# Regrouping the neighbour scores: eight rows with all 64 places per step instead of 32 rows with 16, and the relu of the fourth head on ScalarE

## The chip, the cores and the metric

The kernel runs on one core of one Trainium2 chip. The metric is the device time of one execution in microseconds (us). A core has five engines that run side by side, each through its own instructions in order: TensorE (PE, with its weight loads listed as PEld), VectorE (DVE), ScalarE (ACT), GpSimd (POOL) and SyncE (SP). Sixteen DMA engines move data between HBM and the on-chip memory SBUF. PE writes its results into PSUM, which is divided into eight banks of 2 KB per partition; DVE and ACT read them from there.

## The reference

Two graph layers work on 3327 nodes with 128 features. The adjacency `adj` is a sparse 3327 x 3327 matrix with some 64 non-zeros per row, its diagonal among them. Each layer normalises its input, applies a relu and adds its result to its input. Layer 0 is an attention layer with four heads; layer 1 is a graph convolution with the same adjacency.

```python
def _gatv2_head(x, A_shape, w1, w2, a, Wlin):
    x1 = x @ w1
    x2 = x @ w2
    E = jax.nn.leaky_relu(x1[:, None, :] + x2[None, :, :], negative_slope=0.01)
    s = E @ a
    s = jnp.tanh(s / 8.0) * 8.0
    s = jnp.exp(s) * A_shape
    s = s / jnp.sum(s, axis=-1, keepdims=True)
    out = s @ x @ Wlin.T
    return jax.nn.leaky_relu(out, negative_slope=0.01)
...
# layer 0: x = x + concat(heads) @ w        layer 1: x = x + relu(D^-1/2 (A+I) D^-1/2 (h @ W.T + b))
```

A score is needed only where `A_shape` is not zero. For one row i and one neighbour j, the score of a head is the sum over 128 features of `a * leaky_relu(x1[i] + x2[j])`. The leaky relu is 0.01 times its input plus 0.99 times a relu, and the linear part is a sum of two numbers, one of the row and one of the neighbour. What is left to be done for each pair is the relu of 128 features in four heads.

## The kernel before

The rows are worked on in 26 blocks of 128. A block has two halves of 64 rows (`hb`). For every row, `prep` (L353) finds the column numbers of its non-zeros with MAX8 and MATCH_REPLACE8 on DVE and puts the first 64 into 64 *places*; the few that are left over go into an extra list. The places come in four chunks of 16. `idx` holds for each chunk and each set of eight rows the 128 addresses (8 rows x 16 places) of the table rows to be fetched. A table row holds, besides adjacency values, the features of a node, one partial score per head, and its `x2` for the four heads.

`gather` (L578) fetches: one indirect DMA on POOL (L597) brings 128 table rows into one *tile* `g[:, t]`, one row to a partition. Eight tiles make one buffer `g`; there are four buffers. In the kernel before, a buffer `w` (0 to 3) holds chunk `w` of all 64 rows of the half: tile `t` is rows 8t to 8t+7. The extra entries and the rows' own entries on the diagonal have a buffer of their own, `ge`.

The scores are worked out in *groups* `m`, nine to a half. Groups 0 to 7 are four tiles each, two groups to a buffer; so a group is 32 rows with 16 places. Group 8 is for `ge`. A group goes through these steps:

- `stage_z` (L612): for each pair of heads `hp`, PE transposes the four tiles of both heads (L624, eight transposes) into a PSUM tile `z` of two banks, one per head, in which the columns stand in the order (32 rows, 16 places). DVE then writes `r = max(z, -x1)` for both heads in one instruction of 1024 columns (L640); `x1n` holds `-x1`, and the same number is used for the 16 columns of a row. Since `max(z, -x1)` is `relu(z + x1) - x1`, the score's number of the row, `pex`, makes up for the difference. Two `z` tiles exist, so a `z` can be written again only when its `r` is done.
- `stage_r` (L645), one group later: four matmuls, one per head, multiply `r` with `a` and write into two rows per head of the PSUM tile `s` (L653). The two groups of a buffer fill one `s`.
- `finish` (L657), once per buffer: ACT copies `s` into `ssb` (L662); DVE makes `wq` (L666) from the adjacency values; PE turns `ssb` back (L671); DVE adds the partial scores of neighbour and row (L674, L677); ACT takes tanh and exp (L682, L684); DVE multiplies with `wq` into `wt` (L693); PE adds the weighted features of the neighbours into `ag` (L702). In L702 the eight tiles write into four strips of 32 PSUM partitions each (`cg`), and neighbouring matmuls are for different strips.

After L702 the buffer is free (`allow("g")`), and the next eight gathers may go out on POOL. `close` (L727) finishes a half.

The order of all this is written out by hand. The loop at L1195 emits, for group i, first `stage_z` of group i, then `stage_r` of group i-1. Between the parts it calls `slot()` (L858), six times per group. Each call goes one step further in `finish` and `close` (a `yield` is a step), in the search for the next block's columns (`prep`, with L422, L453, L456 on DVE and the transposes L365 of the adjacency with their ACT copies L367), and sends off gathers (`fetch`, `trickle`). Every engine takes its instructions in that order. A branch at the end that recomputes everything densely is not taken.

## Time and profile before

| What | Number |
|---|---|
| Median of 14 runs | 3397.97 us (3374.82 to 3404.78) |
| The profiled execution | 3400.7 us, span 3399.0 us, instructions 52430 |
| Mean granted TensorE clock | 0.897 |
| Busy: PE / DVE / ACT / POOL | 2652.0 / 2107.0 / 673.5 / 1739.4 us |
| DVE, `r` of groups 0 to 7 (L640) | 832 instructions, 1012.0 us |
| PE, transposes into `z` (L624) | 6656 matmuls, 1048.8 us |
| PE, `ag` (L702) | 3328 matmuls, 206.7 us |
| POOL, gathers of `g` (L597) | 1664, 1615.1 us |
| DMA | 826.94 MB, 619.41 MB of it by POOL's gathers |

The profile is of one execution. "Busy" is the time in which an engine works on an instruction; matmuls overlap one another, and their ends are modelled, so that a busy PE is not PE at its peak. A group of instructions is shown as: line, engine, operation, out<-in, shape, how often, and then the busy time, the mean of one in ns, and the idle time of the engine ahead of it with what ended it. A matmul with 32-bit operands shows as two records (L702: 208 x 8 matmuls, 3328 records); a transpose is one. "Issue" is time in which the engine waited for nothing that the profile shows, and "remote" is a wait whose end the profile can't put down to an instruction.

### The profile page before, as it was taken

To read this page: it belongs to the slowest core of one execution; us is meant where nothing else is said; L and a number is where in the kernel's file an instruction comes from. 1 tells how busy PE (TensorE), PEld (TensorE's weight loads), DVE (VectorE), ACT (ScalarE), POOL (GpSimd) and SP (SyncE) were. 2 spreads that over 40 slices of the span, in tenths; PEclk is the share of its full clock that TensorE was granted. 3 is DMA by queue.
4 is the path that set the end of the run, shared out by engine and by line. 5 is a ranking of instruction groups with operands and counts; after the bars stand their busy time and mean duration, and the time that the engine had idled before them with its cause. 6 is when DMAs were issued, how large, how long until landed. Compare 5 with 4: busy or idle time off the path is not lost.

```text
span 3399.0 us, 52430 instructions
## 1 busy us (share of the span) xinstructions
PE 2652.0 (78%) x19410; PEld 1785.4 (53%) x19410; DVE 2107.0 (62%) x6478; ACT 673.5 (20%) x1703; POOL 1739.4 (51%) x1822
## 2 busy tenths in 40 slices
PE   6578778787777877877778778787788787788887
PEld 4355555555555555555555555555555555555553
DVE  6567666666666666666665665666665666665442
ACT  3122112112211211212221121121121121121110
POOL 3555555555555555555555545555455455455520
PEclk8789888988988988999898888899898899899998
DMA  9977778678778767877767867877776776777896
GB/s 326 310 257 240 219 259 267 217 245 273 224 230 264 247 215 245 270 222 238 263 214 245 263 199 247 269 226 231 241 244 213 239 239 222 239 240 222 262 269 174
DMA packets 417844, 826.94 MB, mean 243 GB/s; under 512 B 38435, under 2 KB 288815, under 8 KB 414255
## 3 DMA queue, kind: packets, MB, share of 16 engines
q0 software_dynamic: 141440, 619.41, 55.8%
q1 hardware_dynamic: 165343, 147.87, 13.8%
q10 hardware_dynamic: 110800, 56.25, 5.7%
q8 instruction: 156, 2.56, 0.3%
q14 instruction: 105, 0.86, 0.1%
HBM read 754.47 MB, written 113.22 MB: 255 GB/s over the span
## 4 chain that ended last, share of the span: by engine, by line
PE 47%; DVE 21%; another core or an unknown queue 14%; issue 8%; DMA 4%; ACT 3%; POOL 1%; ACTq 0%; SPq 0%; DVEq 0%
PE z L624 16%; DVE r L640 10%; PE s L653 9%; PE tr L671 4%; PE z L629 3%; DVE cand L422 2%; PE ag L702 2%; DMA g<-table,idx 2%; PE tr L379 1%; PE ag L721 1%; PE tr L365 1%; POOL g L597 1%; DVE cand L456 1%; ACT r L637 1%
## 5 line engine op out<-in xcount | busy, mean ns | idle before, releaser
L597 POOL DMA_INDIRECT g<-table,idx x1664 | 1615.1, 971 | 1395.4 <-PE ag L702 826.7
L624 PE MATMUL z<-ident,g 128*128 128x128 f32 x6656 | 1048.8, 304 | 305.8 <-DVE r L640 223.0
L640 DVE TENSOR_TENSOR r<-z,x1n 128x1024 f32<-128x1024 f32 x832 | 1012.0, 1218 | 394.6 <-remote 302.5
L624 PEld LDWEIGHTS z<-ident,g 128*128 128x128 f32 x6656 | 861.9, 158 | 530.4 <-DVE r L640 329.2
L653 PE MATMUL s<-r,sel 128*2 128x512 f32 (+1 forms) x3744 | 558.4, 601 | 21.5 <-issue 12.0
L671 PE MATMUL tr<-ident,ssb 128*128 128x128 f32 x988 | 181.8, 311 | 172.5 <-issue 101.4
L662 ACT COPY ssb<-s 128x512 f32<-128x512 f32 x260 | 147.2, 566 | 721.2 <-PE s L653 338.7
L702 PE MATMUL ag<-g,wt 128*32 128x133 f32 x3328 | 206.7, 285 | 86.2 <-issue 82.7
L702 PEld LDWEIGHTS ag<-g,wt 128*32 128x32 f32 x3328 | 121.5, 112 | 259.4 <-issue 242.8
L674 DVE TENSOR_TENSOR sc<-tr,g 128x32 f32<-128x32 f32 x208 | 39.1, 188 | 319.3 <-remote 144.1
L671 PEld LDWEIGHTS tr<-ident,ssb 128*128 128x128 f32 x988 | 123.6, 156 | 208.9 <-issue 123.6
L422 DVE MAX8 cand<-codes 128x8 f32<-128x52 uint16 x1664 | 215.2, 204 | 0.0
L635 DVE TENSOR_TENSOR r<-z,x1n 128x128 f32<-128x128 f32 x104 | 27.6, 287 | 240.7 <-PE s L653 191.3
L682 ACT ACTIVATE th<-sc 128x32 f32<-128x32 f32 x260 | 58.1, 223 | 596.3 <-DVE sc L677 308.6
L367 ACT COPY at<-tr 128x512 f32<-128x512 f32 (+1 forms) x175 | 97.4, 556 | 344.2 <-remote 149.4
L597 POOL DMA_INDIRECT ge<-table,idxo x104 | 100.7, 968 | 113.5 <-PE ag L721 52.1
L653 PEld LDWEIGHTS s<-r,sel 128*2 128x2 f32 x3744 | 58.1, 82 | 185.3 <-issue 176.8
L379 PE MATMUL tr<-at,x_sb 128*128 128x128 f32 x488 | 80.8, 310 | 90.8 <-ACT at L367 65.8
L629 PE MATMUL z<-oi,x1b 128*128 128x256 f32 x416 | 145.4, 431 | 0.0
L453 DVE MAX8 lists<-cand 128x8 f32<-128x272 f32 (+1 forms) x338 | 133.2, 394 | 2.9
L365 PE MATMUL tr<-ident,adjb 128*128 128x128 f32 x676 | 113.0, 291 | 25.2 <-DMA adjb<-in_adj_dram 16.9
L379 PEld LDWEIGHTS tr<-at,x_sb 128*128 128x128 f32 x488 | 67.0, 210 | 115.6 <-ACT at L367 96.1
(201 smaller groups left out, 2624.3 us busy)
## 6 DMA issues: line engine op xcount, KB each, us to landing
adjb<-in_adj_dram SPq DMA_DIRECT2D x26, 1664.0 KB
table<-AT_d SPq DMA_DIRECT2D x26, 1664.0 KB
AT_d<-at ACTq DMA_DIRECT2D x150, 256.0 KB
g<-table,idx POOLq DMA_INDIRECT x1664
table<-img SPq DMA_DIRECT2D x12, 1296.0 KB
adjb<-AT_d SPq DMA_DIRECT2D x72, 128.0 KB
g<-AT_d SPq DMA_DIRECT2D x25, 256.0 KB
g<-AT_d ACTq DMA_DIRECT2D x25, 256.0 KB
```

Of the source, the lines that this page charges most:

```text
L365: nc.tensor.transpose(pt[:, q, :], adjb[:, (j0 + q) * P:(j0 + q + 1) * P], ident)
L379: nc.tensor.matmul(pq[:, :P], x_sb[:, j0 + q, :], at[:, q, :], start=(q == 0), stop=(q == js[-1]))
L422: nc.vector.max(cand[:, c, 8:].rearrange("p (r s) -> p r s", s=32)[:, :, sgm % 32], codes.rearrange("p a b -> p (a b)")[:, sgm % 32 * SEG: ...
L453: nc.vector.max(top, of)
L597: return nc.gpsimd.indirect_dma_start(out=g[:, t, lo:hi], out_offset=None, in_=tab, in_offset=bass.IndirectOffsetOnAxis(ap=at[:, t:t + 1], ...
L624: nc.tensor.matmul(z[:, i, q * P:(q + 1) * P], g[:, m % 2 * 4 + q, c0:c0 + D], ident, is_transpose=True, start=(q == 0 or m < 8), stop=(m ...
L629: nc.tensor.matmul(z[:, i, :n], k.x1b[:, h * D:(h + 1) * D], k.oi[:, hb * n:(hb + 1) * n], start=False, stop=True, skip_group_check=True)
L640: nc.vector.tensor_tensor(r.rearrange("p h (i s) -> p h i s", s=16), z.rearrange("p h (i s) -> p h i s", s=16), k.x1n[:, 2 * hp:2 * hp + 2 ...
L653: nc.tensor.matmul(k.s[32 * h:32 * h + 2, :n], sel[:, h, 31 - at:33 - at], rs[h // 2][:, h % 2, :n], start=(at == 0), stop=(at == 1 or m = ...
L662: nc.scalar.copy(ssb[:, :nk * P], s[:, :nk * P])
L671: nc.tensor.transpose(pt[:, q, :], ssb[:, q * P:(q + 1) * P], ident)
L702: nc.tensor.matmul(ag[32 * cg:32 * cg + 32, u, :WORK], wt[:, t].rearrange("p h q -> p (h q)"), g[:, t, f0:f0 + WORK], start=(w == 0 and t ...
```

## The change

Three things change, in five places.

1. *What a buffer and a group hold.* Buffer `w` now holds all four chunks of 16 rows instead of one chunk of 64 rows. Its tile `4m+q` is chunk `q` of rows 16w+8m to 16w+8m+7. A group is then eight rows with all 64 places. The gathers are as many, and each brings the same 128 table rows as before for its chunk and rows; only the order is different (`own` and `which` in `gather`). In `z` the columns are put in the order (8 rows, 64 places): each transpose writes its 128 columns as eight runs of 16, 64 columns apart. `finish` undoes this when it copies `s` into `ssb` on ACT, by reading `s` in another order.
2. *The relu of the fourth head.* Since one row now has 64 columns next to each other, DVE's instruction for the second pair of heads covers only the third head (512 columns), and ACT does the fourth in eight instructions of 64 columns, `relu(z + x1)` with the row's `x1` as a bias per partition. `prep` makes a second copy of `x1` without the minus sign (`x1p`, on ACT), and `pex` of the fourth head takes the other row score (two DVE instructions instead of one), because that head's `r` no longer lacks `x1`.
3. *The order of the matmuls into `ag`.* A tile's strip is now that of its rows, `(2w+m) % 4`. A buffer holds only two sets of eight rows, so its eight tiles write into two strips instead of four, and neighbouring matmuls alternate between those two.

```diff
--- before.py
+++ after.py
@@ -559,16 +559,19 @@
                 nc.tensor.matmul(pm[:, h * P:(h + 1) * P], w1_sb[:, h, :], hTb, start=True, stop=True)
             x1n = pb.tile([P, H, P], F32, name="x1n")
             nc.scalar.activation(x1n, pm[:, :H * P].rearrange("p (h i) -> p h i", h=H), AF.Copy, scale=-1.0)
+            x1p = pb.tile([P, P], F32, name="x1p")
+            nc.scalar.copy(x1p, pm[:, (H - 1) * P:H * P])
             pmx = pb.tile([P, 16, H], F32, name="pmx")
-            nc.vector.tensor_tensor(pmx, tmask[:, :, None].to_broadcast([P, 16, H]),
-                                    p_all[:, b, None, :H].to_broadcast([P, 16, H]), OP.mult)
+            for h0, h1, of in ((0, H - 1, 0), (H - 1, H, H)):
+                nc.vector.tensor_tensor(pmx[:, :, h0:h1], tmask[:, :, None].to_broadcast([P, 16, h1 - h0]),
+                                        p_all[:, b, None, of + h0:of + h1].to_broadcast([P, 16, h1 - h0]), OP.mult)
             yield
             yield
             pm = bank()
             nc.tensor.matmul(pm[:, :16 * H], modsel, pmx.rearrange("p t h -> p (t h)"), start=True, stop=True)
             pex = pb.tile([P, 16, H], F32, name="pex")
             nc.scalar.copy(pex, pm[:, :16 * H].rearrange("p (t h) -> p t h", h=H))
-            k.x1b, k.x1n, k.pex = x1b, x1n, pex
+            k.x1b, k.x1n, k.x1p, k.pex = x1b, x1n, x1p, pex
             yield
 
         def rows_in():
@@ -588,14 +591,18 @@
                 c0, n0 = (0, FEAT + COLS) if hb == 0 else (FEAT, BODY + FEAT)
                 nc.sync.dma_start(g[:HALF, FOUND, :n0], tables[b % 2][:NP * ROW].rearrange("(r c) -> r c", c=ROW)[rows:rows + HALF, c0:c0 + n0])
             else:
-                g, n, at = rows_in(), WT, k.idx[:, w, WT * hb:WT * hb + WT]
+                g, n, at = rows_in(), WT, k.idx
+
+            t0 = WT * hb + 2 * w
 
             def one(t):
+                own = 8 * (2 * w + t // 4)
+                which = at[:, t % 4, t0 + t // 4:t0 + t // 4 + 1] if w < NW else at[:, t:t + 1]
                 lo, hi = (0, FEAT + COLS) if hb == 0 else (0, BODY + FEAT)
                 if w < NW:
-                    lo, hi = (8 * t, hi) if hb == 0 else (0, BODY + 8 * t + 8)
+                    lo, hi = (own, hi) if hb == 0 else (0, BODY + own + 8)
                 return nc.gpsimd.indirect_dma_start(out=g[:, t, lo:hi], out_offset=None, in_=tab,
-                                                    in_offset=bass.IndirectOffsetOnAxis(ap=at[:, t:t + 1], axis=0))
+                                                    in_offset=bass.IndirectOffsetOnAxis(ap=which, axis=0))
 
             queue.extend((k, hb, w, partial(one, t)) for t in range(n))
             k.g[hb, w] = g
@@ -621,7 +628,8 @@
                     h = 2 * hp + i
                     c0 = k.f0[hb] + PROJ + h * D
                     for q in range(n // P):
-                        nc.tensor.matmul(z[:, i, q * P:(q + 1) * P], g[:, m % 2 * 4 + q, c0:c0 + D], ident,
+                        to = z[:, i, q * P:(q + 1) * P] if m == 8 else z[:, i].rearrange("p (i q s) -> p q i s", q=4, s=16)[:, q]
+                        nc.tensor.matmul(to, g[:, m % 2 * 4 + q, c0:c0 + D], ident,
                                          is_transpose=True, start=(q == 0 or m < 8), stop=(m < 8), skip_group_check=True)
                     if m == 8:
                         nc.tensor.matmul(z[:, i, n:n + HALF], g[:HALF, FOUND, c0:c0 + D], ident[:HALF, :HALF],
@@ -636,9 +644,14 @@
                                             k.x1n[:, 2 * hp:2 * hp + 2, HALF * hb:HALF * hb + HALF], OP.max)
                     nc.scalar.activation(r[:, :, :n], z[:, :, :n], AF.Relu)
                 else:
-                    r0 = HALF * hb + 32 * (m % 2)
-                    nc.vector.tensor_tensor(r.rearrange("p h (i s) -> p h i s", s=16), z.rearrange("p h (i s) -> p h i s", s=16),
-                                            k.x1n[:, 2 * hp:2 * hp + 2, r0:r0 + 32, None].to_broadcast([P, 2, 32, 16]), OP.max)
+                    r0 = HALF * hb + 8 * m
+                    nh = 2 - hp
+                    nc.vector.tensor_tensor(r[:, :nh].rearrange("p h (i s) -> p h i s", s=HALF), z[:, :nh].rearrange("p h (i s) -> p h i s", s=HALF),
+                                            k.x1n[:, 2 * hp:2 * hp + nh, r0:r0 + 8, None].to_broadcast([P, nh, 8, HALF]), OP.max)
+                    if hp:
+                        for e in range(8):
+                            nc.scalar.activation(r[:, 1, e * HALF:(e + 1) * HALF], z[:, 1, e * HALF:(e + 1) * HALF], AF.Relu,
+                                                 bias=k.x1p[:, r0 + e:r0 + e + 1], scale=1.0)
                 out.append(r)
             return out
 
@@ -659,11 +672,15 @@
             f0 = k.f0[hb]
             nt, nk, nm = (WT, 4, 2) if w < NW else (OVT, OVT, 1)
             ssb = ph.tile([P, BANK], F32, name="ssb", bufs=1)
-            nc.scalar.copy(ssb[:, :nk * P], s[:, :nk * P])
+            if w < NW:
+                nc.scalar.copy(ssb.rearrange("p (q i s) -> p q i s", q=4, s=16), s.rearrange("p (i q s) -> p q i s", q=4, s=16))
+            else:
+                nc.scalar.copy(ssb[:, :nk * P], s[:, :nk * P])
             if w < NW:
                 wq = pb.tile([P, WT, 8], F32, name="wq")
-                diag = bass.AP(g.tensor, g.offset + BODY * hb, [list(g.ap[0]), [WIDE + 8, 8], [1, 8]])
-                nc.vector.tensor_tensor(wq, diag, qmask[:, None, :].to_broadcast([P, WT, 8]), OP.mult)
+                diag = bass.AP(g.tensor, g.offset + BODY * hb + 16 * w, [list(g.ap[0]), [4 * WIDE + 8, 2], [WIDE, 4], [1, 8]])
+                nc.vector.tensor_tensor(wq.rearrange("p (m k) q -> p m k q", m=2), diag,
+                                        qmask[:, None, None, :].to_broadcast([P, 2, 4, 8]), OP.mult)
             yield
             yield
             pt = ps_tr.tile([P, 4, P], F32, name="tr")
@@ -674,8 +691,12 @@
             nc.vector.tensor_tensor(sc[:, :nt].rearrange("p (m k) h -> p m k h", m=nm),
                                     pt.rearrange("p k (h m) -> p m k h", m=32)[:, :nm, :nk],
                                     g[:, :, f0 + D:f0 + D + H].rearrange("p (m k) h -> p m k h", m=nm), OP.add)
-            nc.vector.tensor_add(sc[:, :nt], sc[:, :nt], k.pex[:, 8 * hb:8 * hb + 8] if w < NW else
-                                 k.ex[:, OVT * hb:OVT * hb + OVT, 42:42 + H])
+            if w < NW:
+                t0 = WT * hb + 2 * w
+                sc_v = sc.rearrange("p (m k) h -> p m k h", m=2)
+                nc.vector.tensor_tensor(sc_v, sc_v, k.pex[:, t0:t0 + 2, None, :].to_broadcast([P, 2, 4, H]), OP.add)
+            else:
+                nc.vector.tensor_add(sc[:, :nt], sc[:, :nt], k.ex[:, OVT * hb:OVT * hb + OVT, 42:42 + H])
             yield
             yield
             th = pb.tile([P, WT, H], F32, name="th")
@@ -697,10 +718,11 @@
                 yield
                 yield
                 yield
-                for t in range(WT):
-                    u, cg = t // 4, t % 4
-                    nc.tensor.matmul(ag[32 * cg:32 * cg + 32, u, :WORK], wt[:, t].rearrange("p h q -> p (h q)"),
-                                     g[:, t, f0:f0 + WORK], start=(w == 0 and t < 4), stop=False, skip_group_check=True)
+                for q in range(4):
+                    for m in range(2):
+                        t, u, cg = 4 * m + q, (2 * w + m) // 4, (2 * w + m) % 4
+                        nc.tensor.matmul(ag[32 * cg:32 * cg + 32, u, :WORK], wt[:, t].rearrange("p h q -> p (h q)"),
+                                         g[:, t, f0:f0 + WORK], start=(w < 2 and q == 0), stop=False, skip_group_check=True)
                 allow("g")
                 return
             am = pb.tile([P, OVT, HALF], F32, name="am", bufs=1)
```

## The prediction

> **What bounds the kernel now.** I read the page first (busy shares, then the chain that ended last), then the groups of the lines that the change touches, then the waits, and at last a stretch of the middle in 4 us windows and in order of time. The page and its groups:
>
> ```profile
> PE 2652.0 (78%) x19410; PEld 1785.4 (53%) x19410; DVE 2107.0 (62%) x6478; ACT 673.5 (20%) x1703; POOL 1739.4 (51%) x1822
> ...
> PE 47%; DVE 21%; another core or an unknown queue 14%; issue 8%; DMA 4%; ACT 3%; POOL 1%; ACTq 0%; SPq 0%; DVEq 0%
> ...
> L624 PE MATMUL z<-ident,g 128*128 128x128 f32 x6656 | 1048.8, 304 | 305.8 <-DVE r L640 223.0
> L640 DVE TENSOR_TENSOR r<-z,x1n 128x1024 f32<-128x1024 f32 x832 | 1012.0, 1218 | 394.6 <-remote 302.5
> ```
>
> No engine is full. The chain is PE for 47% of the span and DVE for 21%: of PE's 2652 busy us, 0.47 x 3399 = 1598, a share of 0.60, lie on the path; of DVE's 2107, 714 us, or 0.34. These two shares price what lies beside other work and what does not.
>
> More rows that give prices, from the groups by shape and the waits on POOL:
>
> ```profile
> L702 PE MATMUL ag<-g,wt 128*32 128x133 f32 x3328 | 206.7, 285 | 86.2 <-issue 82.7 <-DMA g<-table,idx 1.8
> L635 DVE TENSOR_TENSOR r<-z,x1n 128x128 f32<-128x128 f32 x104 | 27.6, 287 | 240.7 <-PE s L653 191.3 <-remote 27.8 <-PE z L629 19.5
> L637 ACT ACTIVATE r<-z 128x512 f32<-128x512 f32 x104 | 62.0, 601 | 292.6 <-DVE r L635 254.5 <-issue 38.1
> L737 ACT ACTIVATE agn<-ag,rec 128x128 f32<-128x128 f32 x104 | 32.6, 364 | 85.1 <-DVE rec L732 49.0 <-DMA g<-AT_d 21.2 <-issue 3.8
> ...
> POOL g L597 <- PE ag L702: 826.7, 193, 11.2
> ```
>
> The last line says that 193 times POOL waits for `ag` before it sends the next eight gathers. Now the windows (busy us of PE, PEld, DVE, ACT, POOL, then clock, DMA share, GB/s) and some instructions in order of time (start, us, engine):
>
> ```profile
> 1718.00:1722.00 4.00, 4.00 (x49) 3.05 (x48) 2.76 (x8) 1.17 (x2) 1.49 (x2) 1.00 0.08 12
> 1722.00:1726.00 4.00, 3.62 (x32) 2.36 (x31) 3.83 (x14) 1.14 (x5) 3.08 (x4) 1.00 0.80 239
> 1726.00:1730.00 4.00, 3.92 (x24) 2.29 (x23) 1.56 (x7) 0.27 (x1) 3.09 (x4) 1.00 0.88 289
> ...
> 1713.85 1.97 PE L624 MATMUL z<-ident,g 128*128 128x128 f32 x8 [7.20 <-DVE r L640]
> 1713.97 0.63 ACT L737 ACTIVATE agn<-ag,rec 128x128 f32<-128x128 f32 x2 [1.90 <-DVE rec L732]
> 1719.26 0.64 PE L702 MATMUL ag<-g,wt 128*32 128x133 f32 x16
> 1720.20 0.95 POOL L597 DMA_INDIRECT g<-table,idx  x1 [9.79 <-PE ag L702]
> 1722.31 1.04 PE L624 MATMUL z<-ident,g 128*128 128x128 f32 x8
> 1731.80 1.23 DVE L640 TENSOR_TENSOR r<-z,x1n 128x1024 f32<-128x1024 f32 x1 [4.09 <-remote]
> ```
>
> The reader is to see a beat. `ag` ends, POOL sends eight gathers (1720.20 to 1730.17, 1.25 us apart). For 6 us PE and DVE work densely (DVE 3.83 of 4 us). Then DVE stands idle (1.56 of 4 us, and a wait of 4.09 us with no releaser) until POOL's run is over. Laid over one another by their start, the runs of gathers show DVE fully busy from 2.5 to 5.0 us after the start and 0.2 busy from 8 to 11 us. I can't name what stalls PE there; the change leaves POOL's 1664 gathers as they are. The gathers land 12 us or more before PE needs them (worked out from the packets' bytes), so they are not late.
>
> **The change part by part.** The sum is made against the profiled execution, 3400.7 us (span 3399.0 and 1.7 around it), which is 2.7 above the median.
>
> *DVE does 512 columns instead of 1024 for the second pair of heads*, in 26 x 2 x 8 = 416 groups. Width costs (1218 - 287)/896 = 1.04 ns a column (L640, L635), so 512 columns take 686 ns: 0.532 us less, 221 us in all. With the path share 0.34 that is -75. The ends are 0 (the stalls take it all) and -221. What is late next is PE or ACT.
>
> *ACT gets 8 x 416 = 3328 instructions of 64 columns.* Nearest row: L737, 128 columns from PSUM with one number per partition, 364 ns, and a pair in 0.63 us, so the second adds 0.27. L662's widths (588 ns for 512 columns, 479 for 384) give 0.85 ns a column, so 64 fewer save 0.054. Eight take 0.31 + 7 x 0.21 = 1.8 us per group, 750 us in all: ACT goes from 673 to some 1430 busy, 42%, no bound by itself. From below: 1.3 us, by the 0.095 us between the one-column copies L490 to L493; from above: 2.9 us, eight times 364 ns. What counts is whether the relu is late for PE. For each group I took from the trace the end of the last transpose into the second `z`, the end of the ACT instruction that stands ahead of the relu, and the first PE instruction that needs this `z` or `r`. With 1.9 us (a handoff included) 73 of 415 groups are late, by 37 us together, nearly all behind the exp L684; with 1.5 us 13; with 3.0 us 170. With 0.60 that is +22 (8 to 102). Behind the relus in ACT's order stand `ssb`, whose delay the trace's slack before L671 takes up, and the copies L367 and L737, 67 us late in sum with 1.9 us; part of that reaches PE: +10 (0 to 40).
>
> A rule of the Trainium skill speaks against this move: "ScalarE: Activation LUTs", Rules for kernel authors, says to do a relu on VectorE and not on ScalarE. The rows agree that the move is dear (1.8 us on ACT for 0.53 on DVE). By that page's figures (What ACT_TABLE_LOAD costs: 280 ns + 0.833 ns a column with a pointer operand, 93 ns of overlap) my estimate would be 2.0 us for eight, and the sum some 5 us higher.
>
> *The matmuls into `ag` alternate between two strips.* 16 records span 0.64 us though one is 285 ns: four strips run at once, in steps of (0.64 - 0.285)/3 = 0.118 us. With two there are eight steps: 7 x 0.118 + 0.285 = 1.11 us, 0.47 more for each of 208 buffers, 98 us. It is PE time at the very place that releases POOL, so I take 0.60: +59. The ends: L702's own share of the chain (2% of the span, a third of its busy time) +32, and all of it, +98.
>
> *`z` is written in runs of 16 columns.* No row of before writes PSUM that way. DVE reads PSUM with a stride at L674 in 188 ns, as fast as L677 reads in order (194), and the matmuls L754, which read SBUF in runs of eight, take 1.06 us for eight like L765 in order. So I take 0. The other end is a transpose at half speed: eight take 1.97 us instead of 1.04 under the half clock (the rows of 1713.85 and 1722.31), 832 x 0.93 = 774 us; below 0 nothing, as the number of columns is the same.
>
> The Trainium skill has a rule against this, too: "PSUM — Partial Sum Buffer", Specifications, says that any non-contiguous access pattern slows matmuls significantly. It gives no figure, and no run here shows it yet.
>
> *The rest.* `x1p`: 26 ACT copies of at most 0.36 us; the second `pmx` instruction: 26 x 0.22 us on DVE (L563); both lie in `prep` and are put at +5 together (0 to 15). `ssb`, `wq` and `sc` handle as many elements as before, in another order: 0, or +-15 if L666's 45 us changed by its whole size. The gathers: same number, same columns, same `first`; POOL's 0.97 us each do not look at the order: 0. SP's DMAs, hidden behind all this, are untouched.
>
> Sum: -75 + 22 + 10 + 59 + 5 = +21, so 3421.7 in this execution's terms, 3419 on the median: 3420.
>
> **The rivals.**
>
> *DVE is the bound for longer than the chain says* (the other side). For: DVE is fully busy in the stretch before each stall. Against: PE shows as much there, and waits for DVE's `r` only 98 us in waits under 2 us. If 0.8 of the 221 us lie on the path: -177 + 96 = -81, 3317. The point that decides is a share of 96/221 = 0.43.
>
> *The beat is locked to POOL's runs.* For: in more than half of the runs the next gather starts 2.1 to 2.7 us after the run before has ended, so that what DVE saves is spent in the stall. Then the gain is 0 and `ag` counts at each of the 193 waits: 0 + 91 + 37 = +128, 3526.
>
> *ACT's small instructions don't overlap.* 2.9 us per group: +102 instead of +22, and +40 instead of +10: 3529. Against: the pair L737.
>
> *The strided writes slow the transposes.* Even a tenth of 774 us would end at 3496; half of it near 3800.
>
> **How the numbers follow.** The forecast has 0.34, its own range 3380 to 3460; DVE the bound 0.36; the locked beat 0.16; no overlap 0.08; strided writes 0.06. The prices of the two leading cases lie too close together to call more than this; 3420 is kept since the three others all lie above it. From 3285 (a DVE share of 0.95 on the path) to 3570 (the locked beat with the ACT copies and the rest at their upper ends, +168) all but the strided writes and the tails are held. What can be told from no change here is 0.2%, 6.8 us. Faster: 0.03 of the forecast and 0.34 of the rival, 0.37; same: 0.08 and 0.02, 0.10; slower: 0.23 of the forecast and the other rivals' 0.30, 0.53.
>
> **What would show it.** Right: the second `r` on DVE at 0.69 us; the eight relus in 1.7 to 2.0 us; L702's 16 records in 1.1 us; DVE down by 215, ACT up by 750 or less; L624 at 304 ns still. Wrong: PE waiting for the new ACT line for more than 60 us (ACT bounds), L624 longer, or DVE's share of the chain falling well under 21% with a shorter span (DVE was the bound).

## The result, and the profile after

The change made the kernel slower: 3746.35 us (median of 10 runs) against 3397.61 us for the kernel before (47 runs), a ratio of 1.1026 with a 95% interval of 1.1005 to 1.1046. The forecast was 3420 with a range up to 3570; "slower" was its likeliest sign, but the loss of 349 us is twice what the range allowed (172 above the time before).

The page of the changed kernel (line numbers have moved: `z` L632, `r` on DVE L649, the new relus on ACT L653, `ssb` L676 and for group 8 L678, `tr` L688, `ag` L724, gathers L604):

```profile
PE 2804.8 (75%) x19410; PEld 1957.3 (52%) x19410; DVE 1920.7 (51%) x6504; ACT 1369.8 (37%) x5057; POOL 1734.9 (46%) x1822
...
PE 44%; DVE 17%; another core or an unknown queue 14%; ACT 12%; issue 8%; DMA 4%; ACTq 1%; POOL 1%; SPq 0%; DVEq 0%; POOLq 0%
PE z L632 14%; ACT r L653 8%; DVE r L649 8%; PE s L666 5%; PE tr L688 4%; PE z L637 4%; PE ag L724 2%; PE tr L379 2%; DMA g<-table,idx 2%; PE tr L365 2%; DVE cand L456 1%; DMA g<-AT_d 1%; ACT ssb L676 1%; PE ag L743 1%
```

The busy times moved as intended: DVE down by 186 us, ACT up by 696. But the chain that ended last now has ACT for 12% of the span instead of 3%, 8% in the new relus alone. The groups by shape (count, then busy time and mean ns of one, then idle time ahead and what ended it):

```profile
L653 ACT ACTIVATE r<-z,x1p 128x64 f32<-128x64 f32 x3328 | 725.9, 330 | 912.9 <-DVE r L649 549.5 <-issue 180.0 <-DVE cand L456 77.7
...
L649 DVE TENSOR_TENSOR r<-z,x1n 128x512 f32<-128x512 f32 x416 | 284.1, 683 | 161.3 <-PE z L632 118.5 <-remote 27.6 <-issue 6.5
L724 PE MATMUL ag<-g,wt 128*32 128x133 f32 x3328 | 253.9, 286 | 45.8 <-issue 45.2 <-DMA g<-table,idx 0.4
...
L676 ACT COPY ssb<-s 128x512 f32<-128x512 f32 x208 | 130.5, 627 | 24.9 <-remote 20.3 <-PE ag L743 1.9 <-PE s L666 0.9
```

The sizes are the predicted ones (683 ns for DVE's half). New is the end of the first row: ACT stands idle 549.5 us ahead of its relus until DVE has finished *its* half of the same `r`. The last row shows the other side of it. In the kernel before, the same copy and PE's wait for it stood so:

```profile
L662 ACT COPY ssb<-s 128x512 f32<-128x512 f32 x208 | 122.3, 588 | 580.8 <-PE s L653 279.3 <-PE ag L702 154.1 <-remote 82.4
...
PE tr L671 <- ACT ssb L662: 56.9, 55, 5.4
```

Ahead of `ssb` ACT was idle for 580.8 us, 279.3 of them until the scores `s` were there; now it is idle for 24.9, because the scores wait for ACT: 195 of the 260 copies start directly behind a run of relus (within 0.15 us of its end, worked out from the starts and ends). The waits of the changed kernel (us in total, times, longest); in the kernel before the first stood at 826.7 us:

```profile
POOL g L604 <- PE ag L724: 1232.5, 202, 14.5
ACT r L653 <- DVE r L649: 549.5, 216, 8.8
...
PE tr L688 <- ACT ssb L676: 120.4, 76, 7.8
...
PE tr L688 <- ACT ssb L678: 112.0, 33, 4.9
```

POOL waits 406 us longer for `ag` before it sends the next gathers. How the delay gets there can be followed in a stretch of the same trace in order of time (start, us, engine):

```profile
1714.99 0.68 DVE L649 TENSOR_TENSOR r<-z,x1n 128x512 f32<-128x512 f32 x1
...
1715.71 1.74 ACT L653 ACTIVATE r<-z,x1p 128x64 f32<-128x64 f32 x8 [1.95 <-DVE r L649]
...
1717.29 0.53 ACT L678 COPY ssb<-s 128x384 f32<-128x384 f32 x1
...
1717.87 0.55 PE L688 MATMUL tr<-ident,ssb 128*128 128x128 f32 x3 [2.55 <-ACT ssb L678]
```

The relus begin 0.04 us after DVE has ended. Behind them on ACT stands `ssb`, and for `ssb` waits PE's `tr`. In the whole trace not one of the 416 relu runs overlaps DVE's instruction, and 304 begin within 0.1 us of its end (worked out from the starts and ends of the two lines). The second pair of heads takes 2.46 us from DVE's start to ACT's end in the median (2.78 in the mean, as in 112 groups ACT begins later), where DVE alone took 1.22.

### The profile page after: what moved, and what is told of

It is laid out like the page before. It is cut to its first block, busy times and chain, and to the rows that moved or that the text cites. A ratio compares the mean times of both kernels' runs of the same rounds, so it can differ in the third digit from the quotient of the medians.

```text
span 3740.4 us, 56076 instructions
## 1 busy us (share of the span) xinstructions
PE 2804.8 (75%) x19410; PEld 1957.3 (52%) x19410; DVE 1920.7 (51%) x6504; ACT 1369.8 (37%) x5057; POOL 1734.9 (46%) x1822
## 3 DMA queue, kind: packets, MB, share of 16 engines
q14 instruction: 132, 1.08, 0.1%
## 4 chain that ended last, share of the span: by engine, by line
PE 44%; DVE 17%; another core or an unknown queue 14%; ACT 12%; issue 8%; DMA 4%; ACTq 1%; POOL 1%; SPq 0%; DVEq 0%; POOLq 0%
PE z L632 14%; ACT r L653 8%; DVE r L649 8%; PE s L666 5%; PE tr L688 4%; PE z L637 4%; PE ag L724 2%; PE tr L379 2%; DMA g<-table,idx 2%; PE tr L365 2%; DVE cand L456 1%; DMA g<-AT_d 1%; ACT ssb L676 1%; PE ag L743 1%
## 5 line engine op out<-in xcount | busy, mean ns | idle before, releaser
L604 POOL DMA_INDIRECT g<-table,idx x1664 | 1613.5, 970 | 1728.6 <-PE ag L724 1232.5
L632 PE MATMUL z<-ident,g 128*128 128x128 f32 x6656 | 1089.9, 314 | 277.5 <-DVE r L649 164.7
L632 PEld LDWEIGHTS z<-ident,g 128*128 128x128 f32 x6656 | 912.2, 164 | 479.7 <-DVE r L649 250.6
L649 DVE TENSOR_TENSOR r<-z,x1n 128x1024 f32<-128x1024 f32 x832 | 792.1, 953 | 568.8 <-remote 250.7
L653 ACT ACTIVATE r<-z,x1p 128x64 f32<-128x64 f32 x3328 | 725.9, 330 | 912.9 <-DVE r L649 549.5
L688 PE MATMUL tr<-ident,ssb 128*128 128x128 f32 x988 | 192.1, 323 | 405.2 <-ACT ssb L676 120.4
L688 PEld LDWEIGHTS tr<-ident,ssb 128*128 128x128 f32 x988 | 122.9, 159 | 456.1 <-ACT ssb L676 145.9
L724 PEld LDWEIGHTS ag<-g,wt 128*32 128x32 f32 x3328 | 199.8, 115 | 201.8 <-issue 180.2
L724 PE MATMUL ag<-g,wt 128*32 128x133 f32 x3328 | 253.9, 286 | 45.8 <-issue 45.2
L604 POOL DMA_INDIRECT ge<-table,idxo x104 | 98.3, 945 | 113.3 <-PE ag L743 62.2
L637 PE MATMUL z<-oi,x1b 128*128 128x256 f32 x416 | 145.8, 432 | 0.3 <-issue 0.2
L379 PE MATMUL tr<-at,x_sb 128*128 128x128 f32 x488 | 91.4, 341 | 68.6 <-ACT at L367 61.0
L365 PE MATMUL tr<-ident,adjb 128*128 128x128 f32 x676 | 122.0, 309 | 24.8 <-DMA adjb<-in_adj_dram 16.5
L676 ACT COPY ssb<-s 128x512 f32<-128x512 f32 x208 | 130.5, 627 | 24.9 <-remote 20.3
```

The source lines that it names most:

```text
L365: nc.tensor.transpose(pt[:, q, :], adjb[:, (j0 + q) * P:(j0 + q + 1) * P], ident)
L379: nc.tensor.matmul(pq[:, :P], x_sb[:, j0 + q, :], at[:, q, :], start=(q == 0), stop=(q == js[-1]))
L604: return nc.gpsimd.indirect_dma_start(out=g[:, t, lo:hi], out_offset=None, in_=tab, in_offset=bass.IndirectOffsetOnAxis(ap=which, axis=0))
L632: nc.tensor.matmul(to, g[:, m % 2 * 4 + q, c0:c0 + D], ident, is_transpose=True, start=(q == 0 or m < 8), stop=(m < 8), skip_group_check=True)
L637: nc.tensor.matmul(z[:, i, :n], k.x1b[:, h * D:(h + 1) * D], k.oi[:, hb * n:(hb + 1) * n], start=False, stop=True, skip_group_check=True)
L649: nc.vector.tensor_tensor(r[:, :nh].rearrange("p h (i s) -> p h i s", s=HALF), z[:, :nh].rearrange("p h (i s) -> p h i s", s=HALF), k.x1n[ ...
```

## The experiments

The runs were made in five sets, in which the kernel before took 3317, 3317, 2524, 3392 and 2522 us. So a kernel is compared with the kernel before of its own set, by ratio, and a difference in us holds for that set.

**A tile of its own for the output.** The fourth head's relus write a tile `r3`, the third head's half on DVE a tile `r2`; the second pair of group 8 is split in the same way.

```
-  r = pr.tile([P, 2, BANK], F32, name=f"r{hp}")
+  r = [pr.tile([P, BANK], F32, name=f"r{2 + i}") for i in range(2)]      # for hp = 1
...
-  nc.scalar.activation(r[:, 1, e * HALF:(e + 1) * HALF], z[:, 1, ...], AF.Relu, bias=..., scale=1.0)
+  nc.scalar.activation(r[1][:, e * HALF:(e + 1) * HALF], z[:, 1, ...], AF.Relu, bias=..., scale=1.0)
```

> The changed kernel with one thing undone: the relus of the fourth head write a tile of their own, so that nothing in their output is shared with DVE's half. Four theories stand. A: the two halves of the second pair of heads run one after the other because they write one tile, 0.68 us on DVE and then 1.74 us on ACT, and this series holds back `s`, `ag` and the next gathers. B: the matmuls into `ag`, which alternate between two strips (1.08 us instead of 0.64), hold the beat. C: the strided writes of `z` cost. D: the load on ACT by itself costs (727 us more), and `ssb` stands behind it. By A the wait of ACT for DVE's `r` (549.5 us in the sum) falls below 150 us and the kernel comes down to 3400 to 3500 us, 250 us or more below the change's 3746. By B or C it stays above 3600, by D above 3650.

Measured: 3687.41 us, ratio 1.1121 (1.1062 to 1.1179). No gain, so A as stated failed. But its trace shows that the wait had not gone (L658 and L662 are the two halves here):

```profile
ACT r L662 <- DVE r L658: 680.8, 232, 12.3
...
1725.80 0.69 DVE L658 TENSOR_TENSOR r<-z,x1n 128x512 f32<-128x512 f32 x1 [1.86 <-remote]
...
1726.53 1.75 ACT L662 ACTIVATE r<-z,x1p 128x64 f32<-128x64 f32 x8 [4.80 <-DVE r L658]
```

310 of 416 relu runs still begin within 0.1 us of DVE's end and none before it. In the program the first relu still waits for DVE's instruction, although the two now have only the *reading* of `z` in common. The test had not removed what it was meant to remove, and so the sign of D (above 3650), which came true, doesn't tell D from A.

**The parts of the regrouping.** First the regrouping alone, with DVE doing both heads:

```
-  nh = 2 - hp
+  nh = 2
...
-  if hp:
-      for e in range(8):
-          nc.scalar.activation(r[:, 1, ...], z[:, 1, ...], AF.Relu, bias=k.x1p[...], scale=1.0)
```

> The changed kernel's groups of 8 rows with all 64 places are kept, with the strided writes of `z` and the two strips of `ag`, but DVE does both heads of the second pair in one instruction of 1024 columns, as before, and ACT does none. By A (series of DVE and ACT) and by D (ACT's load) what remains is the regrouping alone: 3400 to 3500 us, of which the `ag` order is worth 0 to 98. By B (two strips) 3480 to 3530, the +91 of the locked beat with nothing saved. By C (strided writes) above 3600, near the change itself.

Measured: 3363.59 us, 1.0136 (1.0092 to 1.0181), 46 us. So most of the loss is in the move to ACT. Next, two parts put into the kernel before:

```
-  for t in range(WT):                      # ag
+  for t in (0, 1, 4, 5, 2, 3, 6, 7):
```

> The kernel before, with only the order of the eight matmuls per buffer into `ag` changed, so that neighbours alternate between two strips as in the change. 16 of them should take 1.0 to 1.1 us instead of 0.64, 208 times: 90 to 98 us of PE time. By B it all counts, 3490 us; by the forecast's share of 0.60, 3455 us; by A, C and D it costs less than that, 3400 to 3440 us.

```
+  to = z[:, i].rearrange("p (i q s) -> p q i s", q=4, s=16)[:, q]      # groups 0 to 7
-  nc.tensor.matmul(z[:, i, q * P:(q + 1) * P], g[...], ident, is_transpose=True, ...)
+  nc.tensor.matmul(to, g[...], ident, is_transpose=True, ...)
```

> The kernel before, with only the transposes into `z` written in runs of 16 columns that lie 64 apart, as in the change, and all else as it was, so that the columns of `z` stand in another order than the instructions behind them take them (rows and places are mixed, and the output is not the reference's). By C the transposes take longer than 304 ns and the kernel goes up by 100 us or more; by A, B and D it stays within 20 us of before, and eight transposes still take 1.04 us.

Measured: 1.0007 (0.998 to 1.0033) and 1.0004 (0.9984 to 1.0024). The second settles the strided writes: the transposes take 303 ns as before, and they cost nothing.

```profile
L625 PE MATMUL z<-ident,g 128*128 128x128 f32 x6656 | 1050.6, 303 | 308.3 <-DVE r L641 210.2 <-issue 69.4 <-ACT r L638 8.7
```

The first settled nothing: 16 records took 0.66 us and not the expected 1.0 to 1.1, since in that order each strip still gets only two matmuls a buffer; in the change two strips get four each. That neighbours alternate between two strips is thus not what costs. So the other way round, the regrouping alone with four strips:

```
-  t, u, cg = 4 * m + q, (2 * w + m) // 4, (2 * w + m) % 4
+  t, u, cg = 4 * m + q, m, q               # m is the outer loop here
```

> The regrouping alone, DVE doing both heads, with the matmuls into `ag` sent to four strips in turn, as before the change, and not to two (sums then go to the wrong rows, so that the output is not the reference's). Reordering the kernel before had kept each strip at two matmuls a buffer, and so hadn't made the two-strip case. If the 46 us of the regrouping come from the two strips, 16 records take 0.64 us again instead of 1.08 and the kernel is within 15 us of before; if they come from another part (strided copies, order of the gathers), it stays 30 us or more above.

Measured: 1.0005 (0.9983 to 1.0028). The 16 records of `ag` in order of time, in the regrouping alone:

```profile
1716.30 1.08 PE L718 MATMUL ag<-g,wt 128*32 128x133 f32 x16
```

The same with four strips:

```profile
1701.51 0.64 PE L718 MATMUL ag<-g,wt 128*32 128x133 f32 x16
```

Where each of two strips gets four matmuls of a buffer, they take 1.08 us; where four strips get two each, 0.64 or 0.66. The two strips are the whole price of the regrouping: 208 x 0.44 = 92 us of PE time, of which some 44 us (1.3% of the kernel) count. The order of the gathers and the strided copies cost nothing that can be seen.

**Own tiles on both sides, and the length of the relus.** Now `z` of the third and fourth head lies in tiles of its own, too, in the same four banks:

```
-  z = ps_z.tile([P, 2, BANK], F32, name="z")
+  z = [ps_z.tile([P, BANK], F32, name=f"z{2 + i}", bufs=1) for i in range(2)]    # for hp = 1
```

> In the run with a tile of its own for the output, ACT's relus still began 0.03 us after DVE's instruction ended, every time: the two halves also read one tile, `z`, and are put in a row for that too. Here the third and the fourth head have tiles of their own on both sides, `z` and `r`, in the same memory, so that ACT waits for PE's transposes alone. The regrouping alone was 46 us slower than before, the whole change some 370 on that chip. By A (the series of 0.68 and 1.74 us) what is late is only what 1.74 us on ACT have more than 1.22 on DVE, so that half or more of the gap of 320 us goes: 60 to 210 us above before. By D (ACT's load, 727 us in 3328 small instructions, with `ssb` behind them) it stays 300 us or more above before, with or without the wait.

Measured: 3465.17 us, 1.0477 (1.0426 to 1.0528), 158 us above before: within what A expected. The change with one relu of 512 columns for eight:

```
-  for e in range(8):
-      nc.scalar.activation(r[:, 1, e * HALF:(e + 1) * HALF], z[:, 1, ...], AF.Relu, bias=k.x1p[:, r0 + e:r0 + e + 1], ...)
+  nc.scalar.activation(r[:, 1], z[:, 1], AF.Relu, bias=k.x1p[:, r0:r0 + 1], scale=1.0)
```

> The changed kernel with one ACT instruction of 512 columns in place of the eight of 64 (the first row's value serves all eight rows, so that seven of eight rows get the wrong offset): 0.60 us on ACT instead of 1.74, still in a row behind DVE's 0.68. By A the series is 1.28 us, as long as the 1.22 us of DVE alone, and the kernel comes to 30 to 90 us above before. By the count of ACT's steps (D) it also falls, as ACT's load is 250 instead of 726 us; what tells D from A are the two other runs. If the move of work from DVE to ACT costs by itself, whatever the length (a handoff more on the path), it stays above 150.

Measured: 3472.31 us, 1.046 (1.0423 to 1.0497), 155 us above before. This missed what A expected, and lies where the last case (above 150) had it. In the median the pair takes 1.40 us from DVE's start to ACT's end, only 0.18 more than DVE alone, or 75 us in 416 groups, and yet the kernel is some 107 us slower than the regrouping alone (by the two ratios). The two lengths in a row aren't all. In the mean the pair takes 1.66 us, or 183 us more in 416 groups, as in 84 of them ACT begins more than 0.1 us after DVE's end. And ACT stands still until DVE *comes to* its half, and everything behind the relu on ACT stands with it, as this run's waits show (`ssb` L676 is that of group 8):

```profile
ACT r L652 <- DVE r L649: 789.6, 219, 14.2
...
PE tr L686 <- ACT ssb L674: 140.0, 85, 6.0
...
PE tr L686 <- ACT ssb L676: 66.1, 26, 3.4
```

(In the regrouping alone the two `ssb` ended 55.3 and 11.3 us of PE's waits.) With own tiles and one relu:

> Own tiles for the third and fourth head and one ACT instruction of 512 columns in place of eight (with the first row's value for all eight rows, so seven of eight rows get the wrong offset). So far: regrouping alone +46 us over before, shared tiles and one instruction +155, own tiles and eight instructions +158, shared tiles and eight (the change) some +340. Here DVE's 0.68 us and ACT's 0.69 us lie side by side, shorter than the 1.22 us of DVE alone, and DVE has the change's saving of 220 us. If the length from `z` to a finished `r` is what counts, this is at least as fast as the regrouping alone, -60 to +50 us over before. If each instruction on ACT that PE must wait for costs by itself (a queue in which it stands behind others, and others behind it), it stays 80 us or more above before, whatever its length.

Measured where before took 2524 us: 0.9982 (0.9967 to 0.9997). Since the conditions had changed, this couldn't be set beside the others, so the four kernels were run side by side:

> The change itself, beside the three others under the same conditions. By the series of DVE and ACT it is 10 per cent above before where the kernel before takes 3300 to 3400 us; where the kernel before takes 2524 us and PE is busy nine tenths of the time, the 2.45 us of the series have less idle time of PE to hide in: 7 to 12 per cent.

> Own tiles with eight relus, as run before at 1.048 of before. The same again where before takes 3300 us; 1.03 to 1.06 elsewhere. Against the change itself it should be 4 to 6 per cent faster: that is the series.

> DVE doing both heads, as run before at 1.014 of before, all of it the two strips of `ag`. The same again where before takes 3300 us; where PE is busy nine tenths of the time the 91 us of PE at `ag` count for more: 1.02 to 1.035.

> Own tiles and one relu of 512 columns (seven of eight rows get the wrong offset), as run before at 0.998 of before where before took 2524 us. If the length of the relus is what is left of the loss, it is below DVE doing both heads by 0.5 per cent or more, under these conditions too, by what DVE's shorter work gives back (75 us by the forecast's share); if it is ACT as such, it lies near own tiles with eight relus.

| Kernel (before: 3392.35 us) | us | Ratio (95%) | POOL waits for `ag`, us |
|---|---|---|---|
| regrouping, DVE both heads | 3440.34 | 1.0129 (1.0093 to 1.0165) | 950.6 |
| own tiles, one relu | 3458.36 | 1.0174 (1.0133 to 1.0215) | 947.8 |
| own tiles, eight relus | 3543.18 | 1.0415 (1.0349 to 1.0481) | 1028.4 |
| the change: shared tiles, eight relus | 3736.67 | 1.1012 (1.0978 to 1.1046) | 1224.5 |

The change, own tiles with eight relus (5.4% below the change) and the regrouping lie where they were expected. Own tiles with one relu lie in neither of the two places named: not below the regrouping, and well below own tiles with eight relus. From row to row the time grows by 18, 85 and 193 us, and POOL's wait for `ag` by -3, 81 and 196. (That wait is no measure of the time by itself: it was 530.6 us in the kernel before with `ag` reordered and 745.9 in the regrouping with four strips, which both took as long as the kernel before.) In this order the shared tiles are worth 193 us with eight relus, the length of the relus 85 with own tiles, and DVE's shorter work, with a short relu on ACT in its place, brings nothing: the kernel in which DVE does 207 us less (1903.0 busy against 2109.6) and ACT is short is 18 us *slower* than the one where DVE does it all, with intervals that overlap. The two large shares aren't independent of each other: with one relu, shared tiles cost about 3% (1.046 against 1.0174, from two sets), with eight relus 6%. With own tiles ACT really runs ahead, as this stretch shows (L660 DVE, L664 ACT):

```profile
1729.47 1.23 DVE L660 TENSOR_TENSOR r<-z,x1n 128x1024 f32<-128x1024 f32 x1 [6.09 <-remote]
1729.59 1.74 ACT L664 ACTIVATE r<-z,x1p 128x64 f32<-128x64 f32 x8 [5.78 <-remote]
...
1731.22 0.68 DVE L660 TENSOR_TENSOR r<-z,x1n 128x512 f32<-128x512 f32 x1
```

ACT is through its relus 0.57 us before DVE is through its half; in the change it could only have begun at 1731.9. In 308 of 416 groups ACT now begins before DVE's end, and over all groups its median start is 0.97 us before that end: more than DVE's 0.68, because DVE also does other work ahead of its half. And the waits of PE's `tr`, first with own tiles:

```profile
PE tr L699 <- ACT ssb L687: 93.9, 68, 7.3
...
PE tr L699 <- ACT r L664: 25.9, 22, 1.8
```

The same waits in the run of the change beside it:

```profile
PE tr L688 <- ACT ssb L676: 143.1, 84, 7.7
...
PE tr L688 <- ACT ssb L678: 116.7, 35, 4.9
...
PE tr L688 <- ACT r L653: 50.5, 21, 3.8
```

310 us in the change against 120: the difference, 190 us, is close to the 193 us of the table. Tiles of their own also come free one by one, so that PE could write into one head's `z` earlier, but no gain shows there: PE's transposes into `z` waited 174.3 us for DVE's `r` with own tiles and 171.6 in the change. Own `z` with a shared `r` was not tried, so it isn't known whether `z` alone would have been enough.

**By which way the length costs.** The regrouping alone, and beside it eight relus that nobody waits for, which read a constant:

```
+  idle = ph.tile([P, HALF], F32, name="idle", bufs=1)
+  for e in range(8):
+      nc.scalar.activation(idle, ident[:, :HALF], AF.Relu, bias=ident[:, e:e + 1], scale=1.0)
```

> The regrouping alone, DVE doing both heads, and beside it eight ACT relus of 64 columns per group which read constants and write a tile that nobody reads: ACT's load of the change without its wait and without anyone waiting for it, except what stands behind it in ACT's order (`ssb`, exp, copies). By A it costs little more than the regrouping: 40 to 110 us above before. By D it costs most of the 370: 250 or more.

Measured: 3577.21 us, 1.0787 (1.0756 to 1.0819). Nobody waits for these relus, and yet they cost 216 us over the regrouping alone (by the two ratios), and the waits of this run name `ssb` and the relus in front of it:

```profile
PE tr L686 <- ACT ssb L674: 156.9, 105, 7.7
...
PE tr L686 <- ACT idle L652: 31.5, 15, 6.9
```

(55.3 us for this `ssb` in the regrouping alone.) The 260 us above before are what D expected (250 or more). So ACT's order costs by itself. But this load is larger than the change's: eight of these relus took 3.01 us and not 1.74, as they write the same 64 columns and don't overlap (0.38 us from start to start, 0.35 us each). Four places in turn (`idle[:, e % 4]`) gave 2.01 us:

> The run with idle relus beside the regrouping cost 260 us, but its eight relus all wrote the same 64 columns and took 3.01 us a group instead of 1.74, so ACT had 1155 us of them and not 726. Here they write four places in turn. They should take 1.74 to 1.9 us a group. Still nobody waits for them, but what stands behind them on ACT (`ssb`, exp, copies). If ACT's order behind a long run costs by itself, 80 to 200 us above before (46 of it the regrouping); if only the wait for `r` costs, 40 to 70.

> Own tiles and eight relus as in the run that was 158 us above before, with the copy `ssb` moved from ACT to DVE (208 copies, some 130 us of ACT's time), so that the scores no longer stand behind the relus in ACT's order. If most of what is left of the loss is `ssb` standing behind the relus, it falls to 60 to 110 us above before; if it is the length of the relus themselves, it stays at 130 to 190; if DVE's order is worse for `ssb` than ACT's, it rises.

Both fell into the set where before took 2524 us: 1.0506 (1.0483 to 1.053) and 1.0385 (1.0362 to 1.0408). They were repeated with own tiles and eight relus beside them:

> Own tiles and eight relus with `ssb` on DVE. If `ssb` behind the relus is what the length costs, it is 1.5 to 2.5 per cent faster than own tiles with `ssb` on ACT beside it; if PE's wait for the relu is, within 0.7 per cent of it.

> DVE doing both heads, and eight relus a group on ACT that nobody waits for, in four places in turn (2.0 us a group in the earlier run). What it costs above the 1.013 of the regrouping is what stands behind the relus on ACT: 1.03 to 1.06 of before if that is the way of the loss, 1.013 to 1.02 if it is not.

> Own tiles with eight relus, for comparison: 1.04 to 1.05 of before where before takes 3300 to 3400 us.

Measured, with before at 2522.52 us: `ssb` on DVE (`nc.vector.tensor_copy` for `nc.scalar.copy`) 1.0391 (1.0367 to 1.0414), own tiles 1.0401 (1.0364 to 1.0437), idle relus 1.0498 (1.0471 to 1.0526). Taking `ssb` off ACT changes nothing there, as the second case had it; but DVE, busy for 78% of that run instead of 73%, had to do the copies. What the idle relus cost by themselves can't be read from this set, since no run of the regrouping alone stands beside them, and where before takes 3300 to 3400 us neither of the two was tried. So it is shown that a run of relus on ACT of 3.01 us a group costs through what stands behind it; how much of the 85 us goes that way, and how much through PE's wait for the relus' own result, stays open.

No kernel here that computes the reference is faster than the kernel before.

## Why the prediction was wrong

Term by term, measured in the set of the four:

| Term of the sum | Predicted | Measured |
|---|---|---|
| DVE 512 columns fewer | -75 (0 to -221) | +18, not to be told from 0 (with one short relu on ACT) |
| relu late for PE, copies behind it | +22 and +10 (8 to 142) | +85 for the length, +193 for the shared tiles |
| `ag` in two strips | +59 (32 to 98) | +48 |
| strided `z` | 0 | 0 (1.0004) |
| the rest | +5 | not to be seen |
| Sum | +21 | +344 |

The measured terms are the steps from row to row of that set; in another order the length and the shared tiles would get other shares of their 278 us. That the likeliest sign, "slower", came true is luck for the most part: the forecast's excess came from `ag`, which is 48 of the 344 us.

**The step that failed** is "For each group I took from the trace the end of the last transpose into the second `z`, the end of the ACT instruction that stands ahead of the relu". It lets ACT begin when PE is done. In the program ACT begins when *DVE* is done, since both halves write one `r` and read one `z`. DVE's 0.68 us, and whatever DVE still had to do ahead of them, are missing from that reckoning. The trace of before had shown it, in a row that the prediction quoted for a price: in group 8 DVE and ACT write two parts of one `r` (L635, L637), and ACT's idle time there ends with `DVE r L635`, 254.5 us; in 77 of 104 cases ACT begins within 0.1 us of DVE's end, in none before it. Taken as a wait, and not as a price, it says that the two halves follow one another. The pair then takes 2.46 us instead of 1.22, 516 us in 416 groups; with the share of 0.60 that the prediction used for late work it is +310 in place of +22, and the sum some 3700. Measured for the length and the shared tiles together: 278 us, a share of 0.54.

**A second sentence failed with it**: that the delay of `ssb` is taken up by the slack ahead of the transposes back. That was reckoned for the small delays that the first step had given, and it did not hold for the large ones: PE's wait for `ssb` rose from 57 us to 232 (the rows shown above).

**DVE's saving** was put at its share of the chain, 0.34. Together with a short relu on ACT it was worth nothing, the end that the prediction named with the words "the stalls take it all". With 207 us less work DVE waits as long for ends that the trace can't name (323.1 us ahead of `r` with own tiles and one relu; 329.9 in the regrouping alone). Whether the stalls took the gain, or ACT's 268 us more of work made up for it, these two runs don't tell. A share of the chain says how much of an engine's time lay on the path, not that the path gets shorter when that time is taken away.

**What was right**: the prices of single instructions (0.683 us for 512 columns on DVE against 0.686; eight relus in 1.74 us against 1.8; 1.08 us for `ag` against 1.11; 696 us more on ACT against at most 750); the size of `ag`, inside its bounds, with a share of 0.5 instead of 0.60; nothing for the strided writes. DVE's busy time fell by 186 us and not by 215. The picture behind the price of `ag`, eight steps because neighbours alternate between two strips, was wrong: the kernel before with `ag` reordered alternates in the same way and took 0.66 us; what counted was that a strip gets four matmuls instead of two. The rival of the locked beat fits in that DVE's gain brought nothing, and was wrong in that it counted all of the 91 us at `ag`. The rival of ACT instructions that don't overlap was wrong. Of the signs named, "PE waiting for the new ACT line for more than 60 us" came true (66.0 us of `tr` and 28.8 us of `z` ended with L653). Two readings among the reasons for the rivals don't come out of the trace of before: the pause between two runs of gathers is 2.1 to 2.7 us in 88 of 231 cases, not in more than half, and PE's waits for DVE's `r` under 2 us come to 73 us, not 98. Neither stands in the sum.

On the two rules that were weighed: "ScalarE: Activation LUTs" of the Trainium skill, Rules for kernel authors, sends a relu to VectorE. The direction was right here. By the page's figures (What ACT_TABLE_LOAD costs) the eight relus were an estimated 2.0 us, and 1.74 were measured; that price is not what decided. And "PSUM — Partial Sum Buffer", Specifications (TRN2), has matmuls slowed significantly by a non-contiguous access pattern. For transposes that write runs of 16 columns, 64 apart, this case measured 303 ns against 304, so for these transposes the measurement decides against the rule.

## What to carry to other kernels

Before work is split between two engines, ask which tiles the two halves have in common, on the side that they read as well as on the side that they write: a shared one can put them in a row, and then the lengths add up. A wait for the partner engine in any line of the old profile that is already split this way is the warning. And an experiment that is to remove a wait has to be read in its own trace first: the own output tile alone changed nothing, because the wait was held by the input, too.

## What was not expected of the hardware

*The conditions.* The same kernel (own tiles, eight relus) took 3541.5 us of span in one set and 2619.7 in another. The slower one's page (busy times, granted clock in 40 slices, chain):

```profile
PE 2751.8 (78%) x19410; PEld 1873.0 (53%) x19410; DVE 1905.4 (54%) x6556; ACT 1372.3 (39%) x5115; POOL 1739.7 (49%) x1822
...
PEclk7788999898998998989888889888889889889998
...
PE 49%; ACT 13%; issue 10%; another core or an unknown queue 10%; DVE 10%; DMA 5%; POOL 2%; ACTq 1%; SPq 0%; DVEq 0%; POOLq 0%
```

The faster one's:

```profile
PE 2381.3 (91%) x19410; PEld 1663.6 (64%) x19410; DVE 1900.1 (73%) x6556; ACT 1382.1 (53%) x5115; POOL 1743.4 (67%) x1822
...
PEclk8799999999999999999999999999999999999989
...
PE 56%; ACT 18%; DVE 12%; DMA 8%; issue 3%; ACTq 1%; POOL 1%; SPq 0%; DVEq 0%; POOLq 0%
```

DVE, ACT and POOL are as long busy in both. What is gone in the faster one are the waits without a releaser: 297.8 us on DVE ahead of `r` and 190.1 on ACT ahead of the relus in the slower one, none in the faster one. The mean granted clock is 0.98 against 0.88, and POOL's wait for `ag` 143 us against 1028. So the waits without a releaser, like the stall in the beat that the prediction couldn't name, depend on the conditions and not on the kernel's order alone; what causes them stays open. It isn't the chip alone: on one and the same chip the kernel before took 3317 us in one set and 2524 in another. Prices and shares read under one set of conditions need not hold under the other: own tiles and one relu stand at 1.0174 in one and at 0.9982 in the other.

*Small instructions on ACT.* Eight of 64 columns from PSUM into eight places take 1.74 us, from SBUF into four places in turn 2.01, and into one place 3.01.

*Strips.* Sixteen records of `ag` take 0.64 us over four strips with two matmuls each and 1.08 over two strips with four each; in which order the strips follow one another made no such difference (0.66).
